# Attention over kept tokens with a residual: batch 5's blocks and stores earlier in the last batch, batch 6's outputs all in its second pair, and the last short chunk in four column blocks

## The chip, the cores and the metric

One core of a Trainium2 chip runs the kernel. The metric is the device time of one execution in microseconds (us); the median of several executions is compared. Batches are numbered 0 to 7, so batch 7 is the last one.

## The reference

For every batch, `x` is 512 features by 1024 tokens. A 0/1 mask over the tokens decides which take part.

```python
xt = jnp.transpose(x, (0, 2, 1))
q = xt @ Wq.T                                   # queries, keys and values are all q
qh = q.reshape(B, T, NH, dk).transpose(0, 2, 1, 3)
scores = scale * jnp.einsum('bhqd,bhkd->bhqk', qh, qh)
logits = (scores * cmask + (1.0 - cmask) * NEG) * rmask
attn = jax.nn.softmax(logits, axis=-1)
ctx = jnp.einsum('bhqk,bhkd->bhqd', attn, qh)
out = ctx.transpose(0, 2, 1, 3).reshape(B, T, D) @ Wo.T
x = x + jnp.transpose(out, (0, 2, 1))
```

There are 8 batches, 512 features, 1024 tokens, 8 heads of 64, all in 32-bit floats.

## The kernel before

Masked tokens all get the same output, so the kernel gathers the kept tokens of a batch (at most 544 rows, one of them a mean that stands for the masked ones) and does the attention over those alone. The 544 tokens are five **chunks**: four of 128 and a short one of 32 (`LAST`, index 4; `END` is 32). Two heads are worked together as a **pair**, so a batch has four pairs, 0 to 3, and the program is a run of 32 pairs, written below as (batch, pair). One pair is a loop over five **slots** k = 0 to 4. A slot makes the scores of one chunk of keys (the short chunk in slot 0, then chunks 0 to 3) on TensorE (line 684, line 706 for the short one) and their exponentials on ScalarE (lines 692 and 709), and then runs what the schedule hangs on that slot. The order of instructions on every engine is the order in which this code emits them; nothing reorders it, and only semaphores make an engine wait.

What hangs on the slots, as far as the change touches it:

- `slots_of` (line 1006) lists the work that fills TensorE between scores: the rest of the attention of the pair before (`go_on_attend`, `end_attend`), the turned values (`values`) and their squared lengths (`lengths_of`, then `bias_of`, which gives the exponentials of the next pair their bias), projections of the pair after next, and the output products of the batch before.
- `output(b, i)` (line 874) is the product of chunk i with the output weights: four accumulating matmuls of 512 columns, a copy by ScalarE (line 892), a store to a DRAM scratch `od` on GpSimd's DMA queue (line 894). It does the short chunk as four blocks of 128 columns in four column groups of TensorE, so that 32 rows by 512 columns become 128 partitions by 128 columns. In batch 7 the outputs of batch 6 run in (7,1), slot 3 (chunks 0 and 1) and slot 4 (chunk 2), and in (7,2), slot 1 (chunk 3) and slot 3 (the short chunk).
- Once all of `od` is stored, a batch is finished in eight **blocks**. `load_rows` (line 941, SP's queue) loads the transposed input rows of a block, `fetch` (line 977, GpSimd, an indirect DMA that adds) adds the output rows to them, `finish_blocks` (line 947, VectorE) transposes the sum, and after the eighth block four stores of 512 KB to `out` go onto SP's queue (line 954). Ahead of each `fetch` a one-element copy on GpSimd (`keep_step`, line 974) reads an exponential of the current slot, so that the fetch is not issued before that slot. The tables `ROWS`, `FETCH`, `FINISH` in `late` say in which (pair, slot) each block's step is, for the batch two before the current one; `ROWS_LAST`, `FETCH_LAST` and `FINISH_LAST` do the same in batch 7 for batch 6. The eight buffers of the rows are shared by all batches.
- `invert` (line 835) turns the sums of a pair into reciprocals and sends them through DRAM to all partitions: four small stores and two loads on SP's queue (lines 844 and 849). `contexts` (line 864) multiplies the context of a pair by them, in slot 0 two pairs later.
- In the last pair (7,3) there is no time for that way round: `inverses` (line 819) of (7,2) runs in slot 0, and in slot 1 `spread` (line 803) replicates them by matmuls and ScalarE copies, after which `contexts` of (7,2) follows. `begin_output` (line 898) then makes, for every chunk of batch 7, the product of its first three pairs (in slots 1, 1, 2, 3, 4), copied to SBUF (line 911). After the loop `attend_last` (line 787) does the attention of (7,3) with its own `inverses` and `spread`, and `end_output` (line 914) adds the fourth pair's product to the partial one on VectorE (line 927) and stores the chunk to `od` on SP's queue (line 933). The chunks go in the order 0, short, 1, 2, 3.
- At the very end `fetch_last` (line 957) gathers the eight token blocks of batch 7 from `od` by indirect DMAs on GpSimd (line 963); the first needs chunk 0 and the short chunk in DRAM. `finish_tokens` (line 985) transposes each on TensorE (line 992), adds the input on VectorE (line 993) and stores 256 KB on ScalarE's queue (line 994).

## Time and profile before

| | |
|---|---|
| median of 3 runs | 656.38 us (655.18 to 656.91) |
| the profiled execution | 656.09 us |
| its span, first to last instruction | 654.4 us |
| TensorE matmul busy | 614.3 us (94%) |
| ScalarE busy | 378.3 us (58%) |
| VectorE busy | 359.8 us (55%) |
| GpSimd busy | 211.1 us (32%) |
| DRAM read and written | 72.81 MB and 42.70 MB |

The profiled execution takes 1.7 us more than its span. Busy shares are means over the whole span. The timeline of one engine lists its instructions in order of time, merged when they follow each other: start, busy time, line, operation, what is written from what, how many, and in brackets the idle time before and what ended it. The fp32 matmuls stand as two records each, so `x4` of such a line is two matmuls.

### The profile page before, as it was taken

Reading aid. Unit: us, or ns where it says so; the run is one execution under the profiler, and the core shown is the slowest. Engines: PE = TensorE matmul, PEld = TensorE weight load, DVE = VectorE, ACT = ScalarE, POOL = GpSimd, SP = SyncE. Lnnn points to the kernel's source line nnn. Section 1 sums busy time; section 2 is a strip of 40 time slices with the busy share of each in tenths; the row PEclk is TensorE's granted clock in tenths of the full one; section 3 lists DMA queues with packets and bytes.
Section 4 is the critical chain, followed back from the end, with each engine's and each line's share of the span. In section 5 each row is a group of like instructions: output and inputs, shape, how many; then the busy total and the mean of one; then the engine's idle time right before and its main releaser. Section 6 shows DMA issues by size and latency. Waiting matters only on the chain. (4 is left out here: it accounts for less than half of the span.)

```text
span 654.4 us, 15913 instructions
## 1 busy us (share of the span) xinstructions
PE 614.3 (94%) x6078; PEld 380.5 (58%) x6078; DVE 359.8 (55%) x1034; ACT 378.3 (58%) x1004; POOL 211.1 (32%) x313
## 2 busy tenths in 40 slices
PE   4789799999999999999999999999999999998964
PEld 3756466656665666566665666566665666554323
DVE  6449556335465566746465558566575425444543
ACT  4266558754766577754776577664775556554400
POOL 5620400140067004830176004720275006305422
PEclk7799899999999999999999999999999999999985
DMA  7666612454588757977598756975795635566677
GB/s 237 187 199 166 233 57 67 141 168 133 147 178 214 244 172 186 180 246 230 172 182 257 228 173 155 199 244 187 196 179 164 198 102 94 111 162 188 112 220 219
DMA packets 94543, 116.62 MB, mean 178 GB/s; under 512 B 11911, under 2 KB 61639, under 8 KB 94462
## 3 DMA queue, kind: packets, MB, share of 16 engines
q1 hardware_dynamic: 74030, 75.20, 38.6%
q0 software_dynamic: 16208, 38.25, 25.2%
q10 hardware_dynamic: 4224, 2.10, 1.1%
q8 instruction: 49, 0.80, 0.5%
q14 instruction: 32, 0.26, 0.1%
HBM read 72.81 MB, written 42.70 MB: 177 GB/s over the span
## 5 line engine op out<-in xcount | busy, mean ns | idle before, releaser
L692 ACT ACTIVATE e<-s,bias 128x544 f32<-128x544 f32 x256 | 180.5, 710 | 75.6 <-PE s L684 58.9
L684 PE MATMUL s<-qT 64*64 64x272 f32 x2048 | 154.8, 398 | 6.5 <-ACT e L692 4.9
L748 PE MATMUL av<-e,v 64*64 64x272 f32 x1920 | 132.4, 392 | 0.0
L598 PE MATMUL pq<-xc,wqT 128*128 128x272 f32 x512 | 131.4, 401 | 0.0
L598 PEld LDWEIGHTS pq<-xc,wqT 128*128 128x128 f32 x512 | 93.3, 190 | 36.8 <-issue 21.0
L684 PEld LDWEIGHTS s<-qT 64*64 64x64 f32 x2048 | 77.2, 133 | 55.8 <-ACT e L692 13.4
L883 PE MATMUL po<-woT,cT 128*128 128x512 f32 (+1 forms) x448 | 108.9, 439 | 0.0
L894 POOL DMA_DIRECT2D od<-oc x56 | 30.2, 544 | 238.5 <-ACT oc L892 237.7
L977 POOL DMA_INDIRECT g<-od,block_origin x56 | 90.1, 1610 | 30.9 <-DVE ends L721 8.1
L748 PEld LDWEIGHTS av<-e,v 64*64 64x64 f32 x1920 | 76.6, 134 | 38.1 <-issue 2.1
L664 DVE TENSOR_REDUCE m<-pq 128x1 f32<-128x128 f32 x28 | 8.2, 292 | 132.0 <-ACT qT L610 107.5
L883 PEld LDWEIGHTS po<-woT,cT 128*128 128x128 f32 (+1 forms) x448 | 46.5, 149 | 54.6 <-issue 53.2
L608 ACT COPY qT<-pq 128x272 f32<-128x272 f32 x64 | 24.6, 385 | 69.7 <-PE pq L655 29.0
L947 DVE STREAM_TRANSPOSE xr<-g 128x512 f32<-128x512 f32 x56 | 57.9, 1099 | 7.6 <-DMA g<-od,block_origin 7.5
L645 DVE TENSOR_REDUCE len<-sq 128x10 f32<-128x640 f32 x32 | 25.8, 805 | 60.4 <-ACT sq L643 60.3
L974 POOL COPY step<-e 1x1 f32<-1x1 f32 x75 | 23.7, 316 | 90.7 <-ACT e L692 90.5
L692 ACT ACTIVATION_READ_ACCUMULATOR e<-s,bias 128x1 f32 x256 | 50.5, 197 | 0.0
L544 POOL DMA_INDIRECT xin<-xd,source x40 | 38.7, 968 | 16.6 <-issue 5.6
L892 ACT COPY oc<-po 128x512 f32<-128x512 f32 (+1 forms) x35 | 18.0, 515 | 44.0 <-PE po L883 43.5
L474 DVE STREAM_TRANSPOSE xt<-x 128x1024 f32<-128x1024 f32 x28 | 34.7, 1241 | 1.5 <-DMA xd<-xt 0.9
L532 DVE TENSOR_SCALAR_CACHE_REDUCE junk<-rank,key 128x1024 f32<-128x1024 f32 (+4 forms) x35 | 34.9, 998 | 0.0
L721 DVE CUSTOM_DVE_ANT_0 junk<-el,part 128x272 f32<-128x272 f32 x64 | 27.3, 427 | 6.6 <-ACT el L709 4.4
(175 smaller groups left out, 674.0 us busy)
## 6 DMA issues: line engine op xcount, KB each, us to landing
xd<-xt SPq DMA_DIRECT2D x120, 128.0 KB
x<-in_x_dram SPq DMA_DIRECT2D x56, 256.0 KB
g<-xd SPq DMA_DIRECT2D x56, 256.0 KB
out_dram<-xr SPq DMA_DIRECT2D x28, 512.0 KB
rb<-row SPq DMA_DIRECT2D x60, 160.0 KB
od<-oc POOLq DMA_DIRECT2D x28, 256.0 KB
rank<-ranks SPq DMA_DIRECT2D x6, 512.0 KB
x<-in_x_dram POOLq DMA_DIRECT2D x8, 256.0 KB
```

The source lines that it names most:

```text
L474: nc.vector.transpose(xt.rearrange("p k (d f) -> p k d f", d=ND), xs[b][r][:, :, at : at + n].rearrange("p d (k t) -> p k d t", t=Q),)
L532: nc.vector.tensor_scalar(junk[:, :n], rank[:, i * P :], key[:, col], 0.0, ALU.is_le, ALU.add, accum_out=found[:, col])
L544: nc.gpsimd.indirect_dma_start(out=xin[:n, :], out_offset=None, in_=xds[b], in_offset=bass.IndirectOffsetOnAxis(ap=searches[b][2][:n, i : ...
L598: nc.tensor.matmul(pq[:, :KH], wqT[:, d, pr * P : (pr + 1) * P], xcs[b][:, d, cols], start=(d == 0), stop=(d == ND - 1),)
L684: nc.tensor.matmul(ss[h][r * DK : (r + 1) * DK, hf, :KH], qT[heads[h], c * P + r * DK : c * P + (r + 1) * DK], qT[heads[h], queries[hf]], ...
L692: nc.scalar.activation(e[:, :, h, :], ss[h][:, :, :KH], AF.Exp, bias=bias, scale=SCALE, accum_out=sums[pair[1] % 2][:, h, c : c + 1],)
L721: nc.vector.tensor_tensor_reduce(junk[:, :KH], e[:, 0, h, :], parts[b], 1.0, 0.0, ALU.mult, ALU.add, ends[pr % 2][:, h : h + 1])
L748: nc.tensor.matmul(avs[pair][hf][head, :KH], v[keys, c, head], e[keys, hf, h, :], start=(c == 0 and not crossed), stop=(c == LAST - 1 and ...
L883: nc.tensor.matmul(po[k * n : (k + 1) * n, :w], cTs[b, pr][:, i * P : i * P + n], woT[:, pr, k * w : (k + 1) * w], start=(pr == 0), stop=( ...
L894: nc.gpsimd.dma_start(ods[b][places[i], k * w : (k + 1) * w], oc[k * n : (k + 1) * n, :w])
L947: nc.vector.transpose(xr.rearrange("p (d a) (t i) -> p a d t i", a=A, i=NT)[..., i], gs[b, i].rearrange("p (a d f) -> p a d f", a=A, f=Q),)
L977: nc.gpsimd.indirect_dma_start(out=gs[b, i], out_offset=None, in_=ods[b], in_offset=bass.IndirectOffsetOnAxis(ap=block_origin[:, b, i : i ...
```

## The change

- `begin_output` and `end_output` call a new helper, `add_product`, which does the short chunk as four blocks of 128 columns (as `output` does already), so its ScalarE copy and its VectorE add are 128 partitions by 128 columns in place of 32 by 512, and its one store becomes four of 16 KB, by turns on SP's and on ScalarE's queue.
- The outputs of batch 6 all run in (7,1): chunk 0 in slot 2, chunks 1 and 2 in slot 3, chunk 3 and the short one in slot 4. (7,2) has none left.
- Batch 5's blocks get tables of their own in batch 7: fetches 4 to 7 a little earlier, every block's transposition one to two slots earlier, so that the last is in (7,1), slot 2, where it was slot 4; its four stores go out two in slot 2 and two in slot 3.
- Batch 6's rows are loaded in (7,1) in place of (7,2), its fetches run in (7,2) in place of (7,2) slot 4 to (7,3) slot 1, and its transpositions in (7,3) slots 1 and 2 in place of 1, 2 and 3, so that its four stores follow in slot 2.
- In the last pair `spread` and `contexts` of (7,2) move from slot 1 to slot 0, and the five `begin_output` go to slots 1, 2, 3, 4, 4.

```diff
+    def add_product(b, i, pr, po, start, stop):
+        n = sizes[i]
+        parts = P // n
+        w = D // parts
+        tokens = cTs[b, pr][:, i * P : i * P + n]
+        if parts == 1:
+            nc.tensor.matmul(po, tokens, woT[:, pr, :], start=start, stop=stop)
+            return
+        in_order = woT[:, pr, :].rearrange("p (a d f) -> p d a f", a=A, d=ND)
+        for k in range(parts):
+            nc.tensor.matmul(
+                po[k * n : (k + 1) * n, :w],
+                tokens,
+                in_order[:, k * ND // parts : (k + 1) * ND // parts, :, :],
+                start=start,
+                stop=stop,
+            )
...
     def begin_output(b, i):
         po = bank(f"pa_{b}_{i}")
         for pr in range(ND - 1):
+            add_product(b, i, pr, po, pr == 0, pr == ND - 2)
+        w = D // (P // sizes[i])
...
-        nc.scalar.copy(pa[:n, :], po[:n, :])
+        nc.scalar.copy(pa[:, :w], po[:, :w])
...
     def end_output(b, i):
+        add_product(b, i, ND - 1, po, True, True)
...
+        if parts == 1:
+            nc.vector.tensor_tensor(
+                oc.rearrange("p (d a f) -> p a d f", d=ND, a=A),
+                po.rearrange("p (a d f) -> p a d f", d=ND, a=A),
+                partials[i].rearrange("p (a d f) -> p a d f", d=ND, a=A),
+                ALU.add,
+            )
+        else:
+            nc.vector.tensor_tensor(oc[:, :w], po[:, :w], partials[i][:, :w], ALU.add)
+        for k in range(parts):
+            queue = nc.scalar if k % 2 else nc.sync
+            queue.dma_start(ods[b][places[i], k * w : (k + 1) * w], oc[k * n : (k + 1) * n, :w])
-        nc.sync.dma_start(ods[b][places[i], :], oc[:n, :])
...
         if pr == 1 and b + 1 == B:
-            due = [0, 1]
+            due = [1, 2]
+            do(2, output, b - 1, 0)
...
         elif behind:
-            do(1, output, b - 1, LAST - 1)
             do(1, values, behind)
             do(2, lengths_of, behind)
             do(2, end_attend, before)
             do(3, bias_of, behind)
-            do(3, output, b - 1, LAST)
...
         if pr == 1 and b + 1 == B:
-            do(4, output, b - 1, 2)
+            do(4, output, b - 1, LAST - 1)
+            do(4, output, b - 1, LAST)
         if p + 1 == len(pairs):
             for i in range(NC):
-                do((1, 1, 2, 3, 4)[i], begin_output, b, i)
+                do((1, 2, 3, 4, 4)[i], begin_output, b, i)
...
         FETCH = {(0, 0): (0,), (0, 1): (1,), (0, 2): (2,), (0, 3): (3,), (0, 4): (4,), (1, 0): (5,), (1, 1): (6, 7)}
         FINISH = {(0, 4): (0, 1), (1, 1): (2, 3), (1, 2): (4, 5), (1, 4): (6, 7)}
-        FETCH_LAST = {(2, 4): (0, 1, 2), (3, 0): (3, 4, 5), (3, 1): (6, 7)}
-        FINISH_LAST = {(3, 1): (0, 1, 2), (3, 2): (3, 4, 5), (3, 3): (6, 7)}
+        FETCH_SOON = {(0, 0): (0,), (0, 1): (1,), (0, 2): (2,), (0, 3): (3, 4), (0, 4): (5, 6), (1, 0): (7,)}
+        FINISH_SOON = {(0, 2): (0,), (0, 3): (1,), (0, 4): (2,), (1, 0): (3, 4), (1, 1): (5, 6), (1, 2): (7,)}
+        FETCH_LAST = {(2, 0): (0,), (2, 1): (1, 2), (2, 2): (3, 4), (2, 3): (5, 6), (2, 4): (7,)}
+        FINISH_LAST = {(3, 1): (0, 1, 2, 3), (3, 2): (4, 5, 6, 7)}
-        ROWS_LAST = {(2, 0): (0, 1, 2), (2, 1): (3, 4, 5), (2, 2): (6, 7)}
+        ROWS_LAST = {(1, 0): (0, 1, 2), (1, 1): (3, 4), (1, 2): (5, 6), (1, 3): (7,)}
...
-                if p + 1 == len(pairs):
-                    if k == 1:
-                        spread(before, inv)
-                        contexts(before)
+                if p + 1 == len(pairs) and k == 0:
+                    spread(before, inv)
+                    contexts(before)
...
-                    for i in FETCH.get((pr, k), ()):
+                    for i in (FETCH if b + 1 < B else FETCH_SOON).get((pr, k), ()):
...
-                    for i in FINISH.get((pr, k), ()):
+                    for i in (FINISH if b + 1 < B else FINISH_SOON).get((pr, k), ()):
...
                 while rests:
                     rests.popleft()()
-                    if b + 1 < B:
+                    if b + 1 < B or pr == 1 and len(rests) == 2:
                         break
```

More of the change, by code (lines that the diff above doesn't have):

```diff
@@ L896, in attention_of_kept_tokens @@
     partials = {}
+    def add_product(b, i, pr, po, start, stop):
[15 more added lines that the diff above has]
+            )
     def begin_output(b, i):
-        n = sizes[i]
         po = bank(f"pa_{b}_{i}")
         for pr in range(ND - 1):
-            nc.tensor.matmul(
-                po[:n, :],
-                cTs[b, pr][:, i * P : i * P + n],
-                woT[:, pr, :],
-                start=(pr == 0),
-                stop=(pr == ND - 2),
-            )
+            add_product(b, i, pr, po, pr == 0, pr == ND - 2)
+        w = D // (P // sizes[i])
         pa = sb.tile([P, D], F32, tag="xin", name=f"pa_{b}_{i}", bufs=NC)
-        nc.scalar.copy(pa[:n, :], po[:n, :])
+        nc.scalar.copy(pa[:, :w], po[:, :w])
         partials[i] = pa
@@ L915, in end_output @@
         n = sizes[i]
+        parts = P // n
+        w = D // parts
         if i == 0:
@@ L918, in end_output @@
         po = bank(f"po_{b}_{i}")
-        nc.tensor.matmul(
-            po[:n, :],
-            cTs[b, ND - 1][:, i * P : i * P + n],
-            woT[:, ND - 1, :],
-            start=True,
-            stop=True,
-        )
-        oc = sb.tile([P, D], F32, tag="oc", name=f"oc_{b}_{i}", bufs=NC)
-        nc.vector.tensor_tensor(
-            oc[:n, :].rearrange("p (d a f) -> p a d f", d=ND, a=A),
-            po[:n, :].rearrange("p (a d f) -> p a d f", d=ND, a=A),
-            partials[i][:n, :].rearrange("p (a d f) -> p a d f", d=ND, a=A),
-            ALU.add,
-        )
-        nc.sync.dma_start(ods[b][places[i], :], oc[:n, :])
+        add_product(b, i, ND - 1, po, True, True)
+        oc = sb.tile([P, D], F32, tag="oc", name=f"oc_{b}_{i}", bufs=NC)
+        if parts == 1:
[10 more added lines that the diff above has]
+            queue.dma_start(ods[b][places[i], k * w : (k + 1) * w], oc[k * n : (k + 1) * n, :w])
     def in_blocks(t):
```

## The prediction

> **What bounds the kernel now.** I read the page first, then TensorE's timeline of the last batch, then the timelines of the engines that end TensorE's waits, then the stages of the end in short windows.
>
> ```profile
> PE   4789799999999999999999999999999999998964
> PEclk7799899999999999999999999999999999999985
> ...
> 640.55 5.73 DMA g<-od,origin
> ```
>
> The first two rows are slices of 16.4 us. From the sixth slice to the 36th TensorE is busy nine tenths or more at a granted clock of nine tenths or more: there a microsecond counts only if it is TensorE's own work. The change touches the last seven slices, and the last four have gaps. The third row, from the chain of waits, shows that the end hangs on the gathers of batch 7 out of `od`. So I look for TensorE work and idle time in the last pair, and at what comes between its last product and the first gather.
>
> ```profile
> 576.38 0.64 PE L706 MATMUL s<-qT 64*64 64x272 f32 x8
> ...
> 579.24 3.70 PE L883 MATMUL po<-woT,cT 128*128 128x512 f32 x8
> 582.77 0.60 PE L626 MATMUL v<-ident,qT 128*128 128x128 f32 x4
> 583.61 0.33 PE L626 MATMUL ve<-ident,qT 128*128 128x128 f32 x1 [0.24 <-ACT oc L892]
> 583.87 1.15 PE L684 MATMUL s<-qT 64*64 64x272 f32 x16
> ...
> 588.34 0.32 PE L655 MATMUL top<-ident,top 128*128 128x128 f32 x1 [0.54 <-DVE top L652]
> 588.59 1.08 PE L883 MATMUL po<-woT,cT 128*32 128x128 f32 x32
> 589.60 1.15 PE L684 MATMUL s<-qT 64*64 64x272 f32 x16
> ...
> 597.49 1.13 PE L684 MATMUL s<-qT 64*64 64x272 f32 x12 [0.81 <-ACT el L709]
> 598.56 1.31 PE L810 MATMUL rb<-ident,ris 128*64 128x128 f32 x20
> 599.80 1.98 PE L903 MATMUL pa<-woT,cT 128*128 128x512 f32 x4
> 602.74 3.70 PE L903 MATMUL pa<-woT,cT 128*128 128x512 f32 x8 [0.95 <-DVE cT L867]
> ...
> 615.14 2.76 PE L903 MATMUL pa<-woT,cT 128*32 128x512 f32 x6
> 617.84 1.14 PE L730 MATMUL av<-e,v 128*64 128x272 f32 x8
> 620.28 1.31 PE L810 MATMUL rb<-ident,ris 128*64 128x128 f32 x20 [1.31 <-DVE ris L831]
> ...
> 625.64 4.87 PE L919 MATMUL po<-woT,cT 128*128 128x512 f32 x10
> 631.77 0.27 PE L1403 MATMUL worst_t<-ident,worst 128*1 128x128 f32 x1 [1.26 <-DVE worst L1401]
> 636.69 1.09 PE L992 MATMUL o<-ident,g 128*128 128x128 f32 x4 [4.65 <-DMA g<-od,origin]
> ```
>
> (7,2) begins with its short scores at 576.38, (7,3) near 595.5. From 579 to 626 TensorE is idle in five places: 0.24, 0.54, 0.81, 0.95 and 1.31 us. The short chunk's partial product takes 2.70 us (617.84 less 615.14) though only 32 columns of TensorE work; the same chunk of batch 6, in four column groups and with a fourth pair, takes 1.01 (589.60 less 588.59).
>
> ```profile
> 618.19 1.10 DVE L947 STREAM_TRANSPOSE xr<-g 128x512 f32<-128x512 f32 x1 [0.16 <-DMA g<-od,block_origin]
> ...
> 627.78 0.68 DVE L927 TENSOR_TENSOR oc<-po,pa 32x512 f32<-32x512 f32 x1 [0.28 <-PE po L919]
> ```
>
> ```profile
> 619.32 5.28 SPq L954 DMA_DIRECT2D out_dram<-xr x4
> 627.52 4.07 SPq L933 DMA_DIRECT2D od<-oc x5
> ```
>
> ```profile
> 598.27 1.70 POOL L977 DMA_INDIRECT g<-od,block_origin  x1 [5.82 <-DVE ends L721]
> ...
> 632.96 1.00 POOL L963 DMA_INDIRECT g<-od,origin  x1 [19.56 <-DMA od<-oc]
> ...
> 641.80 0.95 POOL L963 DMA_INDIRECT g<-od,origin  x1 [0.30 <-issue]
> ```
>
> Batch 6's blocks explain two of the waits. VectorE transposes them as they land, until 619.29, and only then inverts the sums of the last pair, for which TensorE waits 1.31 us. Their four stores go out from 619.32, and the stores of `od` follow from 627.52. The short chunk's sum is ready at 628.46, but the gather that needs it starts at 632.96, 4.5 us later.
>
> **The change part by part.** All sums are made against the profiled execution, 656.09 us, of which 654.4 is span.
>
> *1. Outputs of batch 6 from (7,2) to (7,1).* 3.53 us (582.77 less 579.24) and 1.01 us leave (7,2) and enter (7,1): nothing net. (7,1) has no idle time on TensorE, and the sums of batch 6 that chunk 0 in slot 2 needs are ready in its slot 0. The five stores on GpSimd's queue come sooner; nothing but the fetches stands behind them. What the work hid is the price:
>
> ```profile
> 586.51 0.73 ACT L643 ACTIVATE sq<-v 128x640 f32<-128x640 f32 x1
> ```
>
> There are two score buffers, one per head, so the next chunk's scores wait for this chunk's exponentials. Those end 2.6 us after their scores began (586.51 less 583.87; scores take 1.0). Without products between, chunk 1's scores in (7,2) come 1.9 us after chunk 0's (scores, then 0.84 of turned values) and chunk 3's 1.3 to 1.7 us after chunk 2's. The first head's buffer is free 0.9 us sooner than the second's, and I walk the slots: idle of about 0.5 in slot 2, 0.35 for the turned top and 0.45 in slot 4. That is 1.3 in place of 0.24 and 0.54: **+0.5**. Ends: -0.8 (no new wait) and +2.0 (each wait at its full length: 0.7, 1.3 and 0.8).
>
> *2. `spread` and `contexts` of (7,2) from slot 1 to slot 0.*
>
> ```profile
> 594.72 0.18 DVE L832 TENSOR_SCALAR ris<-ends,pads 128x2 f32<-128x2 f32 x1
> ```
>
> The inverses it needs are ready at 594.9, and TensorE is done with the scores of slot 0 at 596.7 (597.49 less 0.81), so `spread` fills the 0.81 us in which TensorE waits for the first exponential. The chain behind it, ScalarE's copies and then VectorE's products, takes 2.9 us from the end of `spread` (602.74 less 599.80). After the change `spread` ends near 597.8, the chain near 600.7, and the third matmul of `pa` of chunk 0 would be due at 600.8: both waits go, **-1.8**. Queued behind the moved chain on VectorE is `add_ends`, which no one needs before the end of the pair. Ends: -1.8 and 0.
>
> *3. The short chunk's partial product in four groups:* twelve matmuls of 128 columns in place of three of 512. By the row at 588.59 sixteen take 1.01 us, so twelve take 0.76: 2.70 becomes 0.76, **-1.9**. The columns are now picked in runs of 32, which no row shows. Ends: -1.9, and +0.2 if the four groups ran one after another (a 512-column matmul is 0.9, a quarter 0.24, twelve 2.9).
>
> *4. Batch 6's blocks sooner.* GpSimd can issue the first fetch when the five `od` stores have landed: (7,2) now begins 4.5 us later, at 580.9, the last store is issued about 582.3 and lands some 2.3 us later, at 584.6. From its first fetch at 598.27 the old order took 20 us to the last landing, so the last lands near 604.6. VectorE is free from 601.8 and needs 8 x 1.1 us: done near 610.6. It then inverts the last sums as soon as ScalarE delivers them, 612 to 613.4, before TensorE asks at 615: **-1.3**. Ends: -1.3 and 0. The rows and batch 5's stores, moved into (7,1) on SP's queue, stand ahead of the small stores and loads of `invert` there; rival D has that. The copies of `keep_step` and the fetches delay on GpSimd only the release of exponential buffers that are used again a pair later.
>
> *5. The short chunk's last product and sum.* One of five products of 0.97 us becomes 0.3, and a sum of 0.68 us on VectorE becomes one of 128 x 128, for which the nearest row is ScalarE's copy of the same shape:
>
> ```profile
> 589.74 0.27 ACT L892 COPY oc<-po 128x128 f32<-128x128 f32 x1 [0.38 <-PE po L883]
> ```
>
> The sum is then ready right behind chunk 0's: 0.7 us sooner, **-0.7**. Ends: -0.9 and 0.
>
> *6. From that sum to the first gather,* 4.5 us now. Three SP issues at 0.39 and two on ScalarE's queue replace two on SP; the last of SP's is issued some 0.9 us after the sum. Then the landing.
>
> ```profile
> L933 SPq DMA_DIRECT2D od<-oc x5: 320/388/1425, 627.5 to 631.3; - x5
> ```
>
> ```profile
> 557.26 1.43 SPq L844 DMA_DIRECT2D row<-rt  x4
> 560.70 1.09 SPq L849 DMA_DIRECT2D rb<-row  x2
> 574.07 5.36 SPq L954 DMA_DIRECT2D out_dram<-xr  x4
> ```
>
> ```profile
> 586.00:588.00 2.00, 1.80 (x32) 0.99 (x24) 0.73 (x1) 1.94 (x6) 0.00 (x0) 1.00 0.05 16
> ...
> 626.00:628.00 2.00, 2.00 (x5) 0.43 (x4) 1.27 (x4) 0.00 (x0) 0.00 (x0) 1.00 0.94 234
> ```
>
> On quiet queues a landing takes 2.0 us (small stores issued by 558.69, their reader at 560.70) to 2.7 us (the gather issued by 633.96, its transposes at 636.69). At 626 to 628 the DMA engines are 94% busy with the block stores. Batch 5's four, issued from 574.07, are drained at 586 (share 0.05 from there): 12 us. Batch 6's, issued at 610.6, are drained at 622.6; chunk 0's sum is ready at about 622.3. So the queues are just quiet: 0.9 + 2.3 = 3.2 us in place of 4.5, **-1.3**. Ends: -1.6 and 0.
>
> The Trainium skill bears on this ("DMA: Bandwidth & Descriptors", Queues, rings and completion order): a completion is signalled only after all earlier writes of that DMA engine, across its queues. The 4.5 us agree; by this rule alone the second queue would bring nothing while block stores drain, and the term would be 0.
>
> Behind the first gather nothing changes in kind: 632.96 to 654.4 is eight gathers 1.25 us apart, their transposes, and stores.
>
> Sum: 0.5 - 1.8 - 1.9 - 1.3 - 0.7 - 1.3 = -6.5, and 656.09 - 6.5 = **649.6 us**. The median of the runs, 656.38, is 0.3 above the profiled execution and within their scatter; I add nothing for it.
>
> **The rivals.**
>
> A, *the clock holds at the end.*
>
> ```profile
> 634.00:636.00 2.00, 0.00 (x0) 0.00 (x0) 0.00 (x0) 0.00 (x0) 1.44 (x2) 0.50 0.44 143
> ```
>
> After TensorE falls idle the granted clock drops to 0.50, and four transposes take 1.09 us where at full clock they took 0.60 (582.77). The gap before them, 4.65 us, shrinks by term 6 to some 3.3. Should the clock hold, the last two groups end 1.0 us sooner: 648.6. Against it: between gathers TensorE would still be mostly idle. The skill ("TensorE: Matmul & The Clock Gate", What's actually happening) has the clock halve after an idle window of about 3.4 us; by that rule either may happen.
>
> B, *the block stores are not drained.* If fetches or transpositions of batch 6 come 2 us or more late, `od` stores meet them, and term 6 goes, with part of 4: 651 to 652. For it: the margin is about nothing.
>
> C, *(7,2) starves.* Term 1 at its far end: 651.1. For it: ScalarE's chain per chunk, 2.6 us, is longer than TensorE's without filler.
>
> D, *slower.* In slot 0 of (7,3) TensorE now waits, in order, for `spread`, behind it VectorE's `contexts` of (7,1), behind that the loads of `invert` on SP's queue, which stand behind batch 5's four stores.
>
> ```profile
> 587.64 1.09 SPq L849 DMA_DIRECT2D rb<-row  x2
> 591.43 0.23 DVE L859 TENSOR_TENSOR rb<-rb 128x64 f32<-128x64 f32 x1 [1.99 <-DMA rb<-row]
> ```
>
> Now they land at 591.4, 17.4 us after the first of those stores is issued (574.07). I expect that store in slot 2 in place of 4, so ahead of slot 3's two products (7.1 us), near 567, and a landing by 587. `spread` waits if it comes after 593, one for one: the first store would have to go out after 576 to cost anything, and near 585 to make the kernel slower by 2 us: 658 or more. Against it: that is later than now, though each transposition is one slot or two earlier.
>
> E, *the end doesn't move,* because something other than the first gather's release sets it: 656. Against it: the gathers follow each other without a wait from 632.96.
>
> **How the numbers follow.** Forecast (648.4 to 650.8): 0.55. A: 0.08. B: 0.17. C: 0.10. E: 0.06. D: 0.04. The range takes in all near ends (-0.8 - 1.8 - 1.9 - 1.3 - 0.9 - 1.6 = -8.3: 647.8) and B with most of C (652.6); about 0.12 is left out. 0.3%, or 2 us, is about what a measurement of this kernel can tell from no change. Faster by more: 0.90 (forecast, A, B, C); within it: 0.06; slower: 0.04.
>
> **What would show it.** (1) In (7,2) a few waits of TensorE for exponentials, each under 1 us. (2) `rb` matmuls directly behind the short scores of (7,3), no wait for `cT`. (3) The short `pa` in about 0.8 us. (4) No wait for `ris`; block stores issued about 15 us ahead of the first gather. (5, 6) First gather about 3 us behind the short chunk's sum, near 626.5. I am wrong if fetches land late, if strided columns make the short products slow, or if (7,1) gets waits.

## The result

| | before | after |
|---|---|---|
| median | 655.78 us (652.07 to 658.79, 6 runs) | 648.82 us (646.89 to 651.73, 6 runs) |
| the profiled execution, its span | 656.09, 654.4 us | 648.79, 647.0 us |
| TensorE matmul busy | 614.3 us (94%) | 614.5 us (95%) |

The ratio on record is 0.9908 with a 95% interval of [0.9883, 0.9934] (the two medians divide to 0.9894): the change takes 0.7 to 1.2% off. The forecast was 649.6 us, the range 647.8 to 652.6. One of ten executions of the kernel with late block stores, below, took 3316 us in a slow state and is left out of that kernel's median.

To see where it comes from I cut the end of the program at points that all kernels here have: **A** the short scores of (7,1) start, **B** those of (7,2), **C** those of (7,3), **D** the first matmul of the last pair's own context, **E** the last product of chunk 0, **F** the short chunk's sum is ready, **G** the first gather of batch 7 starts, **H** the span ends. Start times come from the timelines (F is the sum's start and its busy time). In us:

| kernel | A at | A-B | B-C | C-D | D-E | E-F | F-G | A-G | G-H |
|---|---|---|---|---|---|---|---|---|---|
| before | 552.38 | 24.00 | 19.16 | 22.30 | 7.80 | 2.82 | 4.50 | 80.58 | 21.44 |
| after | 550.25 | 28.80 | 15.52 | 18.49 | 6.27 | 2.06 | 3.49 | 74.63 | 22.12 |

The point A is needed because the two profiled executions differ before they get there. The first lines of the short scores of (7,0) and (7,1), from TensorE's timeline of the kernel before and then of the changed one:

```profile
538.88 0.69 PE L706 MATMUL s<-qT 64*64 64x272 f32 x8
...
552.38 0.69 PE L706 MATMUL s<-qT 64*64 64x272 f32 x8
```

```profile
536.75 0.69 PE L706 MATMUL s<-qT 64*64 64x272 f32 x8
...
550.25 0.69 PE L706 MATMUL s<-qT 64*64 64x272 f32 x8
```

(7,0) takes 13.50 us in both, but starts 2.13 us apart, ahead of everything that was changed. In the runs below A lies anywhere from 548.6 to 553.7. So of the 7.4 us between the two spans 2.13 are scatter of the start, 5.95 come between A and G, and 0.68 are given back behind G. Between A and G kernels with the same instructions agree within some 0.4 us (B-C of the eight kernels that have the same (7,2) is 15.37 to 15.75), which is why the experiments are read there; a timed ratio is uncertain by 1.4 us or more.

**The profile after.** TensorE's timeline of the changed kernel, columns as before:

```profile
582.93 1.60 PE L684 MATMUL s<-qT 64*64 64x272 f32 x14 [0.26 <-ACT e L692]
...
587.67 0.32 PE L655 MATMUL top<-ident,top 128*128 128x128 f32 x1 [0.16 <-DVE top L652]
588.23 1.83 PE L684 MATMUL s<-qT 64*64 64x272 f32 x16 [0.23 <-ACT e L692]
...
594.85 0.84 PE L706 MATMUL s<-qT 64*64 64x272 f32 x6
595.62 1.31 PE L810 MATMUL rb<-ident,ris 128*64 128x128 f32 x20
...
597.94 2.85 PE L905 MATMUL pa<-woT,cT 128*128 128x512 f32 x6
...
612.27 0.86 PE L909 MATMUL pa<-woT,cT 128*32 128x128 f32 x24
613.06 1.14 PE L730 MATMUL av<-e,v 128*64 128x272 f32 x8
614.03 1.26 PE L810 MATMUL rb<-ident,ris 128*64 128x128 f32 x20
...
619.33 1.12 PE L905 MATMUL po<-woT,cT 128*128 128x512 f32 x2
620.39 0.42 PE L909 MATMUL po<-woT,cT 128*32 128x128 f32 x8
...
628.70 1.09 PE L1006 MATMUL o<-ident,g 128*128 128x128 f32 x4 [3.58 <-DMA g<-od,origin]
```

The waits for the first exponential, for `cT` and for `ris` are gone: `rb` stands right behind the short scores, the products of chunk 0 are one line of six, and the second `rb` has no bracket. The short chunk's partial product takes 0.79 us (613.06 less 612.27) where it took 2.70. In (7,2) three waits remain, two for ScalarE's exponentials and one for VectorE's turned top (587.67), and the waits for exponentials are larger than their brackets say. Grouped by line and shape for the slots of (7,2), with count, busy us and mean ns, the scores of the changed kernel and then of the one before:

```profile
L684 PE MATMUL s<-qT 64*64 64x272 f32 x64 | 6.2, 399 | 0.5 <-ACT e L692 0.5
```

```profile
L684 PE MATMUL s<-qT 64*64 64x272 f32 x64 | 4.5, 396 | 0.0
```

The mean matmul is the same, yet the group is "busy" 1.7 us longer: it spans the pauses between one head's scores and the next's, as in the line of 1.83 us at 588.23 where 16 records need 1.1.

VectorE, the queues of SP, ScalarE and GpSimd (one fence each), and the windows of 2 us at the end:

```profile
600.56 7.62 DVE L961 STREAM_TRANSPOSE xr<-g 128x512 f32<-128x512 f32 x8
...
611.94 0.18 DVE L832 TENSOR_SCALAR ris<-ends,pads 128x2 f32<-128x2 f32 x1
...
621.11 0.28 DVE L944 TENSOR_TENSOR oc<-po,pa 128x128 f32<-128x128 f32 x1
```

```profile
608.20 5.27 SPq L968 DMA_DIRECT2D out_dram<-xr  x4
621.21 3.45 SPq L947 DMA_DIRECT2D od<-oc  x6
```

```profile
621.42 0.83 ACTq L947 DMA_DIRECT2D od<-oc  x2
```

```profile
584.03 1.70 POOL L991 DMA_INDIRECT g<-od,block_origin  x1 [3.04 <-ACT e L692]
...
597.20 1.56 POOL L991 DMA_INDIRECT g<-od,block_origin  x1 [0.26 <-issue]
624.88 1.00 POOL L977 DMA_INDIRECT g<-od,origin  x1 [26.12 <-DVE worst L1416]
```

```profile
618.00:620.00 2.00, 2.00 (x14) 0.72 (x10) 0.52 (x2) 0.00 (x0) 0.00 (x0) 1.00 0.32 84
620.00:622.00 2.00, 2.00 (x13) 0.83 (x12) 1.06 (x4) 0.00 (x0) 0.00 (x0) 1.00 0.00 0
```

Batch 6's fetches run from 584.03, VectorE does its eight transpositions in one go from 600.56, the last sums are inverted at 612, before TensorE asks at 614.03, and the four block stores go out 16.7 us ahead of the first gather. By 620 the DMA engines are still (share 0.00; the kernel before has 0.94, 0.92 and 0.89 in the three windows from 626 to 632). The first gather starts 3.49 us behind the short chunk's sum (621.39). That its line names `worst` as its releaser is only the latest semaphore in sight: in the run with chunk 0 sooner, below, the same gather starts at 624.98 and the flag's `worst` is computed only from 625.02 on.

### The profile page after: what moved, and what is told of

It is laid out like the page before. It is cut to its first block, busy times and chain, and to the rows that moved or that the text cites. A ratio compares the mean times of both kernels' runs of the same rounds, so it can differ in the third digit from the quotient of the medians.

```text
span 647.0 us, 15975 instructions
## 1 busy us (share of the span) xinstructions
PE 614.5 (95%) x6102; PEld 382.2 (59%) x6102; DVE 359.0 (55%) x1034; ACT 378.0 (58%) x1004; POOL 211.6 (33%) x313
## 3 DMA queue, kind: packets, MB, share of 16 engines
q10 hardware_dynamic: 4320, 2.13, 1.1%
## 4 chain that ended last, share of the span: by engine, by line
PE 90%; DMA 3%; ACT 2%; issue 1%; DVE 1%; POOL 1%; SPq 1%; POOLq 0%; ACTq 0%
PE s L684 21%; PE pq L598 19%; PE av L748 17%; PE po L883 17%; PE av L730 4%; PE s L706 3%; PE xc L557 3%; PE v L626 2%; PE pa L905 2%; ACT e L692 2%; DMA g<-od,origin 1%; DMA x<-in_x_dram 1%; DMA woT<-in_L_cond_Wq_dram 1%; POOL g L977 1%; PE warm L432 1%
## 5 line engine op out<-in xcount | busy, mean ns | idle before, releaser
L988 POOL COPY step<-e 1x1 f32<-1x1 f32 x77 | 26.5, 344 | 86.2 <-ACT e L692 86.1
```

## The experiments

The theory at this point: each of the six terms is a stall or a piece of TensorE work of its own, and the six add up. The rival: all of it is the quiet DMA queues at the end, and the work saved upstream is only waited for elsewhere. Each experiment undoes one part. All stretches, with the timed median, the ratio to the kernel before and its interval (the kernel before had a median of 655.43 us beside the first four experiments and the last two, 654.59 beside the others; the ratios are those on record and not quotients of the medians):

| kernel | A-B | B-C | C-D | D-E | E-F | F-G | A-G | G-H | us | ratio |
|---|---|---|---|---|---|---|---|---|---|---|
| after | 28.80 | 15.52 | 18.49 | 6.27 | 2.06 | 3.49 | 74.63 | 22.12 | 648.82 | 0.9908 [0.9883, 0.9934] |
| short chunk whole | 28.80 | 15.68 | 20.39 | 6.27 | 2.82 | 2.42 | 76.38 | 21.87 | 650.99 | 0.992 [0.989, 0.9949] |
| `spread` late | 28.80 | 15.41 | 20.50 | 6.27 | 2.06 | 3.50 | 76.54 | 21.16 | 651.6 | 0.9942 [0.9913, 0.9972] |
| outputs back | 24.00 | 19.18 | 18.56 | 7.58 | 2.05 | 5.79 | 77.16 | 21.95 | 653.43 | 0.996 [0.9936, 0.9985] |
| stores late | 28.80 | 15.70 | 18.49 | 6.27 | 2.05 | 6.00 | 77.31 | 22.92 | 654.53 | 0.9967 [0.9939, 0.9995] |
| clock kept | 28.79 | 15.39 | 18.49 | 6.27 | 2.05 | 3.51 | 74.50 | 21.60 | 650.2 | 0.9927 [0.9906, 0.9948] |
| chunk 0 sooner | 28.80 | 15.75 | 18.49 | | | 3.02 | 75.13 | 22.42 | 649.91 | 0.9939 [0.9912, 0.9965] |
| short output in (7,2) | 27.79 | 16.13 | 18.49 | 6.27 | 2.05 | 3.50 | 74.24 | 22.68 | 648.82 | 0.9924 [0.9896, 0.9951] |
| block stores behind | 28.81 | 15.37 | 18.49 | 6.27 | 2.05 | 3.35 | 74.34 | 27.18 | 654.36 | 1.0009 [0.9983, 1.0035] |
| one store | 28.80 | 15.44 | 18.49 | 6.27 | 2.82 | 2.42 | 74.24 | 22.10 | 648.58 | 0.9924 [0.9889, 0.9958] |
| four sums, one store | 27.79 | 16.12 | 18.53 | 6.27 | 2.95 | 2.50 | 74.16 | 21.89 | 648.88 | 0.9918 [0.989, 0.9946] |

**The short chunk whole again** (partial product, last product, sum and store as before).

```diff
     def begin_output(b, i):
...
-            add_product(b, i, pr, po, pr == 0, pr == ND - 2)
+            nc.tensor.matmul(po[:n, :], cTs[b, pr][:, i * P : i * P + n], woT[:, pr, :], ...)
     def end_output(b, i):
...
-        for k in range(parts):
-            queue = nc.scalar if k % 2 else nc.sync
-            queue.dma_start(ods[b][places[i], k * w : (k + 1) * w], oc[k * n : (k + 1) * n, :w])
+        nc.sync.dma_start(ods[b][places[i], :], oc[:n, :])
```

> The changed kernel with the short chunk of the last batch in one piece again (its partial product, its last product, its sum and its single store as before). The measure is the stretch from the start of the short scores of (7,1) to the end of the span: 102.0 us before, 96.75 after. If the sum of terms holds: the partial product goes from 0.8 back to 2.7 us (+1.9), the sum is ready 0.7 later, and the stretch grows by 2.3 to 2.8 us, to about 99.3. Rival, that all of the gain came from clearing the DMA queues of batch 6's stores: no change, 96.8.

C-D grows by 1.90 us: term 3 to the digit. E-F grows by 0.76 us, as term 5 said, but F-G shrinks by 1.07. VectorE's and GpSimd's lines of that run:

```profile
626.33 0.68 DVE L946 TENSOR_TENSOR oc<-po,pa 32x512 f32<-32x512 f32 x1 [0.28 <-PE po L938]
```

```profile
629.43 1.00 POOL L982 DMA_INDIRECT g<-od,origin  x1 [27.73 <-DVE oc L946]
```

The sum is ready at 627.01 and the gather starts 2.42 us later; with four small stores it takes 3.49. So from E to G the whole short chunk is 0.31 us faster (5.24 against 5.55): the four-block end gains nothing. From A to the end of the span the run takes 98.25 us, 1.5 more than the changed kernel, where I had expected 2.3 to 2.8; the 1.07 us are the difference.

**`spread` and `contexts` in slot 1 again.**

```diff
-                if p + 1 == len(pairs) and k == 0:
+                if p + 1 == len(pairs) and k == 1:
                     spread(before, inv)
```

> The changed kernel with spread and contexts of (7,2) back in slot 1 of the last pair. Sum of terms: the waits for the first exponential (0.8) and for cT (0.95) come back in the last pair, the stretch from the short scores of (7,1) to the end grows by 1.5 to 1.8 us, to about 98.4. Rival (all from the DMA queues): no change, 96.8.

C-D grows by 2.01 us, and both waits are back on TensorE:

```profile
595.11 1.13 PE L684 MATMUL s<-qT 64*64 64x272 f32 x12 [0.86 <-ACT el L709]
...
600.22 1.12 PE L905 MATMUL pa<-woT,cT 128*128 128x512 f32 x2 [0.82 <-DVE cT L867]
```

A-G is 1.91 us longer, 1.75 in the run before. (To the end of the span, as the expectation counts, it is 0.95, because G-H came out 0.96 us shorter.) The queues at the end are as quiet in both as in the changed kernel (E-G 5.56 and 5.24), so the rival that all gain lies in them falls.

**The outputs of batch 6 back** in (7,1) and (7,2) as before, with the fetches and transpositions of before.

```diff
         if pr == 1 and b + 1 == B:
-            due = [1, 2]
-            do(2, output, b - 1, 0)
+            due = [0, 1]
...
+            do(1, output, b - 1, LAST - 1)
...
+            do(3, output, b - 1, LAST)
...
-            do(4, output, b - 1, LAST - 1)
-            do(4, output, b - 1, LAST)
+            do(4, output, b - 1, 2)
...
+        FETCH_LAST = {(2, 4): (0, 1, 2), (3, 0): (3, 4, 5), (3, 1): (6, 7)}
+        FINISH_LAST = {(3, 1): (0, 1, 2), (3, 2): (3, 4, 5), (3, 3): (6, 7)}
```

> The changed kernel with batch 6's outputs, fetches and transpositions where they were before (two outputs in (7,2), fetches from slot 4 of (7,2) on, transpositions in slots 1, 2, 3 of (7,3)); the rows, batch 5's steps, spread and the short chunk stay changed. Sum of terms: (7,1) and (7,2) together get shorter by 1.2 (the filler hides waits again), the wait for the last inverses comes back (+1.3 to 1.5), the landing of the od stores takes 1.0 longer, and the tail gives 0.7 back: the stretch is 97.0 to 97.8, only little longer than after. Rival (all from the DMA queues): most of the gain is gone, 100.5 or more.

A-B and B-C together are 1.14 us shorter: that is what term 1 costs. The wait for the last inverses is back, and D-E is 1.31 us longer:

```profile
617.65 1.31 PE L810 MATMUL rb<-ident,ris 128*64 128x128 f32 x20 [1.08 <-DVE ris L832]
```

F-G, which I had expected to grow by 1.0 us, grows by 2.30, from 3.49 to 5.79. The expected whole (97.0 to 97.8, measured 99.11) was too low for that reason, and because G-H did not give 0.7 back. The next run asks for this alone.

**Only the block stores of batch 6 late:** the eighth transposition and the four stores after the last inverses, so that no one waits for `ris`.

```diff
         inv = inverses(pair)
+        finish_blocks(B - 2, NT - 1)
+        while rests:
+            rests.popleft()()
...
-        FINISH_LAST = {(3, 1): (0, 1, 2, 3), (3, 2): (4, 5, 6, 7)}
+        FINISH_LAST = {(3, 1): (0, 1, 2, 3), (3, 2): (4, 5, 6)}
```

> The changed kernel with the last of batch 6's transpositions behind the last inverses, so that its four 512 KB stores go out about 5 us later, some 8 us ahead of the first od store as before the change; TensorE's work and waits stay. Theory: the first gather starts 4.5 us behind the short chunk's sum in place of 3.5 (DMA engines still draining), and the tail behind it is up to 0.7 shorter, so the stretch grows by 0.3 to 1.0. Rival, that the landing got shorter for another reason (two queues, smaller pieces): the distance stays 3.5 and the stretch is unchanged.

SP's queue, GpSimd's and a window of that run:

```profile
615.97 5.27 SPq L971 DMA_DIRECT2D out_dram<-xr  x4
624.01 5.43 SPq L950 DMA_DIRECT2D od<-oc  x6
```

```profile
630.18 1.00 POOL L980 DMA_INDIRECT g<-od,origin  x1 [28.65 <-DMA od<-oc]
```

```profile
624.00:626.00 2.00, 2.00 (x6) 0.76 (x4) 1.31 (x3) 0.00 (x0) 0.00 (x0) 1.00 0.92 201
```

All stretches up to F are those of the changed kernel, and F-G is 6.00 us in place of 3.49: with the DMA engines 92% busy the gather that waits for the same small stores starts 2.5 us later, where I had expected 1.0. Most of it comes before the stores have left their queues. The issues of `od` grouped by queue (shortest, median and longest in ns), in this run and then in the changed kernel:

```profile
L950 SPq DMA_DIRECT2D od<-oc x6: 319/359/2058, 624.0 to 629.1; - x6
L950 ACTq DMA_DIRECT2D od<-oc x2: 363/1138/1914, 624.2 to 624.6; - x2
```

```profile
L947 SPq DMA_DIRECT2D od<-oc x6: 320/350/428, 621.2 to 624.3; - x6
L947 ACTq DMA_DIRECT2D od<-oc x2: 357/392/427, 621.4 to 621.8; - x2
```

On each queue one small store is held for about 2 us in its issue. With the trace's times of every issue and of the signals of each store (16 of them), F-G comes apart into three pieces, in us:

| kernel | sum to last small store issued | to its last signal | to the gather | F-G |
|---|---|---|---|---|
| before (one store) | 1.45 | 2.27 | 0.78 | 4.50 |
| short chunk whole (one store) | 0.35 | 1.29 | 0.78 | 2.42 |
| after (four stores) | 1.12 | 1.45 | 0.92 | 3.49 |
| outputs back (four) | 2.55 | 2.32 | 0.92 | 5.79 |
| stores late (four) | 2.81 | 2.27 | 0.92 | 6.00 |

So of the 2.5 us that block stores in flight cost here, 1.69 are issues held up and 0.82 a later signal; for the one store of the kernel before it is 1.10 and 0.98. The hold is no wait for data (the sum was ready at 624.18), so the statement in the section on the kernel before, that only semaphores make an engine wait, does not hold for these issues. The Trainium skill ("DMA: Bandwidth & Descriptors", Queues, rings and completion order) has a completion signalled only behind all earlier writes of the same DMA engine, across its queues; the later signal (2.27 us in place of 1.45) fits that, but no run here shows it engine by engine, and the held issue is something else.

**Chunk 0's last product sooner.** A theory of mine on the 3.49 us: the first gather waits for chunk 0's 256 KB, not for the short chunk. So chunk 0's last product, sum and store move into the last pair's attention, ahead of the second half of the other head.

```diff
     def attend_last(pair):
...
+                if hf == 1 and c == 1:
+                    end_output(B - 1, 0)
...
-        for i in (0, LAST, *range(1, LAST)):
+        for i in (LAST, *range(1, LAST)):
             end_output(B - 1, i)
```

> The changed kernel with chunk 0's last product, sum and store moved into the middle of the second half of the last attention, so that chunk 0 is stored about 1.5 us sooner and the short chunk's sum some 0.4 later. From the start of the last attention's products to the first gather it is 11.8 us now. Theory (new, from the run with the short chunk whole): the first gather waits for chunk 0's 256 KB to land, 3.4 to 3.7 us after its sum, and not for the short chunk; then this stretch shrinks by 0.3 to 0.6, to about 11.3. Rival, that the four small stores of the short chunk set it: it grows by 0.4, to 12.2. The stretch behind the first gather gets no longer in either case.

```profile
618.80 0.69 DVE L939 TENSOR_TENSOR oc<-po,pa 128x512 f32<-128x512 f32 x1 [1.48 <-PE po L907]
621.67 0.29 DVE L946 TENSOR_TENSOR oc<-po,pa 128x128 f32<-128x128 f32 x1 [0.55 <-PE po L911]
```

```profile
624.98 1.00 POOL L979 DMA_INDIRECT g<-od,origin  x1 [26.36 <-DVE oc L939]
```

Chunk 0's sum is ready at 619.49, 6.60 us behind D (8.13 in the changed kernel, 621.19 less 613.06), and the gather is not sooner: it starts 12.09 us behind D (11.82 in the changed kernel), 3.02 behind the short chunk's sum. The theory fell: the small stores set it. Chunk 0's store no longer stands ahead of them on SP's queue, and the gather follows their sum 0.5 us sooner than in the changed kernel: their place in the queue is worth that much of the 3.49.

**One store for the short chunk,** with the partial product still in four column groups: ScalarE copies its blocks side by side into 32 rows, and the last product, sum and store are whole.

```diff
     def begin_output(b, i):
...
-        nc.scalar.copy(pa[:, :w], po[:, :w])
+        for k in range(parts):
+            nc.scalar.copy(pa[:n, k * w : (k + 1) * w], po[k * n : (k + 1) * n, :w])
     def end_output(b, i):
...
-        add_product(b, i, ND - 1, po, True, True)
+        nc.tensor.matmul(po[:n, :], cTs[b, ND - 1][:, i * P : i * P + n], woT[:, ND - 1, :], ...)
...
-        for k in range(parts):
-            queue = nc.scalar if k % 2 else nc.sync
-            queue.dma_start(ods[b][places[i], k * w : (k + 1) * w], oc[k * n : (k + 1) * n, :w])
+        nc.sync.dma_start(ods[b][places[i], :], oc[:n, :])
```

> The short chunk's partial product stays in four column groups, ScalarE copies it out of its four blocks into one of 32 rows, and the last product, its sum and its store are again one of 512 columns, one sum of 32 x 512 and one store of 64 KB. Theory (the four small stores give back what the shorter product and sum gain): chunk 0's last product to the first gather as in the kernel with the whole chunk, 5.2 to 5.3 us in place of 5.55, with the sum ready 2.8 us behind the product in place of 2.06 and the gather 2.4 behind the sum in place of 3.5; the stretch before stays as in the changed kernel (last pair's chunk 0 partial product to the first contexts 18.5); so short scores of (7,1) to first gather 74.3. Rival (the 2.4 us there came from the later end of the whole partial product and not from the store): sum at 2.8, gather 3.5 behind it, 6.3 in all, first gather at 75.4.

```profile
619.70 0.68 DVE L948 TENSOR_TENSOR oc<-po,pa 32x512 f32<-32x512 f32 x1 [0.28 <-PE po L937]
```

```profile
622.80 1.00 POOL L984 DMA_INDIRECT g<-od,origin  x1 [25.81 <-DVE oc L948]
```

Sum ready at 620.38, gather 2.42 us later, E-G 5.24, C-D 18.49, A-G 74.24: the theory, to 0.06 us. The 2.42 us belong to the one store and not to anything earlier.

**Four sums, one store.** The last product keeps its four groups, four sums of 32 x 128 put the blocks side by side, one store follows. This kernel has the short chunk of batch 6 in (7,2) as the one after next.

```diff
-            nc.vector.tensor_tensor(oc[:, :w], po[:, :w], partials[i][:, :w], ALU.add)
-        for k in range(parts):
-            queue = nc.scalar if k % 2 else nc.sync
-            queue.dma_start(ods[b][places[i], k * w : (k + 1) * w], oc[k * n : (k + 1) * n, :w])
+            for k in range(parts):
+                rows = slice(k * n, (k + 1) * n)
+                nc.vector.tensor_tensor(
+                    oc[:n, k * w : (k + 1) * w], po[rows, :w], partials[i][rows, :w], ALU.add
+                )
+        nc.sync.dma_start(ods[b][places[i], :], oc[:n, :])
```

> With chunk 3 of batch 6 back in (7,2), and the short chunk's last product still in four column groups; four sums of 32 x 128 write their blocks side by side into 32 rows, and one store of 64 KB takes the place of four of 16 KB on two queues. Theory (the number of stores decides): the sums are ready 0.4 to 0.7 us later than the one of 128 x 128 (2.5 to 2.8 behind chunk 0's last product in place of 2.05), the gather 2.4 behind them in place of 3.5: 4.9 to 5.2 in all in place of 5.55, and short scores of (7,1) to first gather 73.6 to 73.9 in place of 74.24. Rival (the place of the last store in its queue decides and not the number of stores): gather 3.3 to 3.5 behind the sums, 5.9 to 6.2 in all, 74.6 to 74.9.

The text on record calls the output that goes back to (7,2) chunk 3; it is the short one.

```profile
620.74 1.17 DVE L946 TENSOR_TENSOR oc<-po,pa 32x128 f32<-32x128 f32 x4
```

```profile
624.41 1.00 POOL L979 DMA_INDIRECT g<-od,origin  x1 [20.87 <-DVE worst L1418]
```

The gather follows the last sum (621.91) by 2.50 us, so one store is 1.0 us quicker than four here as well. But the four sums take 1.17 us and not the 0.7 to 1.0 that the expectation implies, and of the 0.3 to 0.6 us expected only 0.10 are left (E-G 5.45).

**The clock kept at the end,** for rival A: 22 matmuls of no use on the identity while the first gather is in flight, and three between the later groups.

```diff
         fetch_last(B - 1)
+        warm(22, ident)
         for i in range(NT):
             finish_tokens(B - 1, i)
+            if i + 1 < NT:
+                warm(3, ident)
```

> The changed kernel with idle transposes added on TensorE behind the end (22 ahead of the first token block, 3 between blocks; results unused), to keep the granted clock up while the gathers run. Rival A of the prediction (the clock at the end costs time): four transposes take about 0.6 us in place of 1.09 and the stretch from the first gather to the end (21.2 to 22.1 us in the runs so far) shrinks by about 1 us. Theory that DMA and the gathers' issue set that stretch: transposes faster, the stretch unchanged within 0.5.

```profile
630.42 0.63 PE L1006 MATMUL o<-ident,g 128*128 128x128 f32 x4 [1.19 <-DMA g<-od,origin]
```

Four transposes take 0.63 us in place of 1.09, as at full clock, and G-H is 21.60 us, inside the 21.16 to 22.68 that the same tail has without it. The clock at the end is worth nothing that can be seen, and the row shows that the transposes still wait for a gather; a gain below that scatter of 1.5 us is not excluded by this run.

**The short output of batch 6 in (7,2)** as filler, for term 1.

```diff
         elif behind:
+            do(1, output, b - 1, LAST)
             do(1, values, behind)
...
             do(4, output, b - 1, LAST - 1)
-            do(4, output, b - 1, LAST)
...
-        FETCH_LAST = {(2, 0): (0,), (2, 1): (1, 2), (2, 2): (3, 4), (2, 3): (5, 6), (2, 4): (7,)}
+        FETCH_LAST = {(2, 2): (0, 1, 2), (2, 3): (3, 4, 5), (2, 4): (6, 7)}
```

> The changed kernel with only the short chunk's output of batch 6 moved back from (7,1) to slot 1 of (7,2), ahead of the turned values, and batch 6's fetches from slot 2 of (7,2) on. Theory (term 1: without filler TensorE waits for exponentials): (7,1) and (7,2) together, 44.3 us now, get shorter by 0.4 to 0.7, and the block stores still go out at most 1 us later. Rival, that the missing filler is not what lengthens (7,2): 44.3 as now. If the fetches come too late the block stores go out over 2 us later and the way from the last chunk-0 product to the first gather grows past 6 us.

```profile
606.85 5.27 SPq L968 DMA_DIRECT2D out_dram<-xr  x4
```

A to C is 43.92 us in place of 44.32 (43.91 in the other kernel with this filler, 44.18 to 44.55 in the eight with an empty (7,2)): one microsecond of filler there gives back some 0.4 of the 1.16. The block stores still go out 57.57 us behind A (57.95 in the changed kernel), early enough; F-G is the same 3.50. The time is that of the changed kernel within the measurement.

**The block stores behind everything,** on SP's queue after the `od` stores: if only the order counted, this would be as good as draining them.

```diff
-                while rests:
+                while rests and not (b + 1 == B and pr == 3):
                     rests.popleft()()
...
             end_output(B - 1, i)
+        while rests:
+            rests.popleft()()
         issue_stores()
```

> The changed kernel with batch 6's four 512 KB stores held back on SP's queue until the od stores of batch 7 are issued. Theory: the way to the first gather stays 5.5 us (nothing in front of the od stores), but the stretch behind it, where the DMA engines are busy 0.5 to 1.1 of the time, grows by 5 to 9 us, since 2 MB more have to pass. Rival, that the issue of the gathers (1.25 us apart) sets that stretch: it grows by less than 2.

SP's queue and a window of that run, and the window of the changed kernel at the same place:

```profile
620.60 3.45 SPq L947 DMA_DIRECT2D od<-oc  x6
624.10 17.46 SPq L968 DMA_DIRECT2D out_dram<-xr  x4
```

```profile
640.00:644.00 4.00, 0.46 (x3) 0.06 (x1) 0.90 (x2) 0.00 (x0) 0.00 (x0) 0.91 1.10 320
```

```profile
640.00:644.00 4.00, 1.09 (x4) 0.71 (x4) 1.28 (x2) 0.00 (x0) 0.00 (x0) 0.50 0.64 183
```

Up to G nothing gets longer (F-G 3.35), and from G to H it takes 27.18 us, 5.1 more, with the DMA engines busier late (share 1.10, where the changed kernel has 0.64). The whole gain is lost, ratio 1.0009. But this is not the price of 2 MB beside the gathers. The line at 624.10 hides a gap; SP's queue later on, and what that queue waited for (in all, times, longest):

```profile
640.42 1.13 SPq L968 DMA_DIRECT2D out_dram<-xr  x2
```

```profile
SPq L968 <- DMA out_dram<-x: 15.7, 2, 15.3
```

Two of the four stores go out at once. The other two wait up to 15.3 us, because the trace has their issues wait for semaphores that stores of batch 7's tokens (`out_dram<-x`) signal, and are issued only at 640.42 and 641.20. The token stores beside the first two start later (9.27 us behind G in place of 5.67), but the last of them is issued 17.10 us behind G, as in the changed kernel (17.01). The 5.1 us come behind it: the span ends 10.1 us after that issue in place of 5.1. So the expected 5 to 9 us came out for another reason than expected, and what 2 MB cost that move beside the gathers alone stays open.

## Why the prediction was right

The sum, -6.5 us, is close to what the runs show: -5.95 from A to G in the profiles, and a median 6.96 lower (by the interval 4.3 to 7.7). Terms 2, 3 and 4 held, and term 1 was 0.66 us too small. Terms 5 and 6 came out near their sum, but undone one at a time they are off by 1.0 and 0.8 us with opposite signs, so part of the closeness is luck.

| term | predicted | measured | from |
|---|---|---|---|
| 1, outputs into (7,1) | +0.5 | +1.16 | A-C, before to after; -1.14 with them put back |
| 2, `spread` to slot 0 | -1.8 | -2.0 | C-D, `spread` late |
| 3, short partial product in four groups | -1.9 | -1.9 | C-D, short chunk whole |
| 4, batch 6's blocks sooner | -1.3 | -1.3 | D-E, outputs back |
| 5, short chunk's last product and sum | -0.7 | -0.8 to its sum, +0.3 to the gather | E-F, before to after; E-G, short chunk whole and one store |
| 6, sum to first gather | -1.3 | -1.0; -2.1 without the four stores | F-G, before to after; E-G, before to short chunk whole |

*Term 1* was mis-sized, inside its ends: the mechanism, (7,2) without filler waits for exponentials, is in the scores' group of 6.2 us against 4.5, and (7,2) comes out 0.90 us longer than its moved work explains (15.52 against 19.16 less 4.54), (7,1) 0.26. *Terms 2, 3, 4* went as walked, term 4 with time to spare: eight transpositions in a row took 7.62 us, where I had 8 x 1.1, and the block stores went out at 608.20 and not at 610.6. Twelve matmuls of 128 columns picked in runs of 32 took 0.79 us, against 0.76 from the row of contiguous-order products in batch 6, so the unknown of term 3 cost nothing, and the far end of +0.2 (groups one after another) is out.

*Term 5 is where the reasoning failed.* "The sum is then ready right behind chunk 0's: 0.7 us sooner" is true (0.76), but I booked that as time at the gather. The gather waits for the last of four stores. That is the third issue on SP's queue, behind chunk 0's: it is through at 622.51, 1.12 us behind the sum, and the gather starts 2.37 later. One store is through 0.35 us behind the sum, and the gather follows 2.07 later. So 0.77 of the 1.07 us are the wait for the queue; the rest, 0.16 up to the last signal and 0.14 from there to the gather, none of my runs explains. I had counted those issues in term 6 (0.9 and a landing of 2.3: 3.2 against 3.49 measured), but as a part of a gain, without asking what a single store would do on the same quiet queues. The Trainium skill ("DMA: Bandwidth & Descriptors", Issuing engines are not separate DMA queues) says that issuing on several engines saves only the sequencer's time, which is usually small; here that time, 0.4 us for each issue, makes up most of the difference.

*Term 6* missed the price of an issue under the block stores. The row of `od` issues that I showed, 320/388/1425, has it: the 1425 ns are the short chunk's own store, and I read only the median. With one store on quiet queues F-G would have been 2.42 and not 3.2, a gain of 2.1 us where my far end was 1.6; the four stores took half of that back. Put together, terms 5 and 6 gave -1.77 against the -2.0 booked. Of the 4.5 us, which I took to agree with completion order, 1.45 had passed before the store was issued.

Of the rivals, **A** is out: the clock did not hold, four transposes took 1.09 us behind a gap of 3.58 as they did behind 4.65, and holding it moves nothing that stands out of the scatter of G-H. **B** did not happen, the queues were at 0.00 from 620 on, 1.4 us ahead of the first small store; its price from A to G, 2.7 us in the run with late stores, is more than the 1.4 to 2.4 I gave it. **C** happened by half: +1.16 of +2.0. **D** did not: `rb` of (7,3) stands behind the short scores without a wait. **E** is out as far as G is concerned: the end follows the first gather at 21.2 to 22.9 us in all kernels but the one that adds stores behind it. That scatter, 1.5 us with the very same instructions (21.16 and 22.68), is the part that none of my runs explains, and the 0.68 us that the profiled pair gives back there lies within it.

No variant is measurably better than the changed kernel: one store, the short output in (7,2), and that output with four sums and one store save 0.4 to 0.5 us from A to G and come out at 648.6 to 648.9 us.

## What to carry to other kernels

A stall that TensorE shows in its own row can be taken at face value when its work moves: terms 2, 3 and 4 came out within 0.2 us. What ends on a DMA must be priced as a whole, from the last result over the number of issues to the reader: halving the work in front of a store is lost if the store then becomes four. And look where bulk stores drain: the same 2 MB cost nothing when they are gone before the last small store, 2 to 2.5 us when they are in flight under it, and 5 when half of them are issued only with the last token stores. Read the issues one by one: a merged line, or a median, hid a held issue twice here.

## What was not expected of the hardware

- Four stores of 16 KB, two each on two queues, let their reader start 3.0 to 3.5 us behind the sum; one of 64 KB lets it start 2.4 to 2.5 us behind, in three kernels.
- A small store under 2 MB of others lets its reader start 2.1 to 2.5 us later, though the first of the bulk was issued 8.0 us and the last 2.8 us ahead of the first `od` store (615.97 and 621.24 against 624.01). More than half of it is the issue itself: 1.4 to 2.1 us in place of 0.32 to 0.43, on SP's queue and on ScalarE's.
- A vector add of 32 x 128 takes 0.28 us, as long as one of 128 x 128 (0.28): four of the one cost four times the other.
